# Sums of weights times the norm's shift taken as single columns, buffers zeroed at other places, and two steps of a long prologue in another order

## The chip, the cores and the metric

The kernel runs on one core of one Trainium2 chip. The metric is the device time of the whole launch in microseconds (us), the median of three runs. A core has TensorE (PE in the profile, with PEld for its weight loads), VectorE (DVE), ScalarE (ACT), GpSimd (POOL) and SyncE (SP, which here only issues transfers). All five run their own instruction streams and wait for one another by semaphores.

## The reference, cut to what matters

Two layers in float32 on a batch of 16 images of 192 channels and 56x56 points. The first is a Swin block: layer norm, attention in shifted windows of 7x7 with 6 heads of 32, a projection, a second layer norm and an MLP of 768 hidden channels. The second is a depthwise 3x3 convolution whose taps are computed from the pooled image (it isn't touched by the change).

```python
h = _ln(transpose(x, (0, 2, 3, 1)), norm1_g, norm1_b)      # over the 192 channels
h = roll(h, (-3, -3), axis=(1, 2))
win = windows_of_7x7(h)                                    # (16*64, 49, 192)
q, k, v = split(win @ qkv_w + qkv_b);  q = q * 32 ** -0.5
attn = q @ k.T + rel_bias[REL_IDX] + mask                  # mask: windows cut by the roll
out = softmax(attn) @ v @ proj_w + proj_b
x1 = x + roll_back(out)
y = gelu(_ln(x1, norm2_g, norm2_b) @ fc1_w + fc1_b) @ fc2_w + fc2_b
x2 = x1 + y
# then the dynamic depthwise convolution of x2
```

_ln(x, g, b) is (x - mean) / sqrt(var + 1e-5) * g + b. The kernel takes the mean, g and b out of the loop: with W the weights behind the norm, g goes into the rows of W once (the "fold"), the mean over the channels is taken out of the columns of the folded W once (the "centre"), and what b contributes, the sum over the channels of W[c, n] * b[c], is a constant for each column n that is added to the bias. That constant is what the kernel calls the shift. Of the norm itself there remains only one factor per token, 1/sqrt(var + eps).

## The kernel before, as far as the change and the steps touch it

The work is cut into 64 steps: four to an image, each of 7 rows of the upper half of the image and the same 7 of the lower half (T = 7 * 56 = 392 tokens a half). A software pipeline starts with a long prologue (steps 0 and 1, a part of step 2, and all weights), then comes a loop `for i in range(2, NS + 2)`, and an end. The edits all lie in the prologue. A tile has a place of its own or shares one by its tag; PSUM is cut into four pairs of banks, numbered 0 to 3, and `banks(name, k)` takes pair k as soon as those who used it before are done.

The helpers for the weights. The shift is a row: the vector be is spread over 128 columns and is the stationary operand, the raw weights stream past, and every row of the result is the sum. ACT copies row 0 out of PSUM, and `turn_row` then makes columns of it by products with a 1x1 operand.

```python
def fold_scale(raw, g, dst, groups):
    for to, lo, n, factor in groups:
        for c in range(2):
            d, r = dst[:, c, to : to + n], raw[:, c, lo : lo + n]
            if factor == 1.0:
                nc.vector.tensor_scalar(d, r, g[c], None, ALU.mult)
            else:
                nc.vector.tensor_scalar(d, r, g[c], factor, ALU.mult, ALU.mult)

# [...]
def shift(dst, raw, n, be, name):


    for c in range(2):
        cs = slice(c * n // 2, (c + 1) * n // 2)
        mm(dst[:, c, : n // 2], be[0].broadcast_to([128, 128]), raw[:, 0, cs], True, False)
        mm(
            dst[:, c, : n // 2],
            be[1][0:64].broadcast_to([64, 128]),
            raw[0:64, 1, cs],
            False,
            True,
        )
    row = one.tile([1, 2, n // 2], F32, tag="o", name=name)
    nc.scalar.copy(row, dst[0:1, :, : n // 2])
    return row.rearrange("o c n -> o (c n)")

def turn_row(dst, row, lo, n):
    mm(dst, row[:, lo : lo + n], ident[0:1, 0:1], True, True)
```

The start of the program, with the loads and the two tables for the attention scores: rel_r (the relative bias as each window token sees it, loaded by 14 small transfers, 7 for each of two windows) and mask_t. `biases` adds the two and so makes bias_t, which the first scores need. `norm_squares` squares x, `norm_stats` sums x and its squares over the channels on PE, `norm_vars` makes the variance, `norm_root` the root; the factors of step 0 are spread over the partitions by a product (pd), those of later steps by a trip through DRAM (`norm_spread`: rows out, dv back in, both by transfers). `norm1_scale` multiplies x by the factors into the window tiles win0 and win1.

```python
# [...] constants, loads of x and of the weights
nc.sync.dma_start(mask_t, win_mask)

side = 2 * WS - 1
for j in range(2):
    for yq in range(WS):
        q = j * 64 + yq * WS
        nc.gpsimd.dma_start(
            rel_r[q : q + WS].rearrange("p (y x) h -> p y (x h)", y=WS),
            bass.AP(
                rel_bias.tensor,
                yq * side * HEADS,
                [[HEADS, WS], [side * HEADS, WS], [1, WS * HEADS]],
            ),
        )
nc.gpsimd.memset(win0, 0.0)
nc.gpsimd.memset(win1, 0.0)
rel_hk = rel_r[:, ::-1, :].rearrange("p k h -> p h k")
# [...] rel_hk, biases()
g1, be1, bq, bk, bv = columns(*rows1, 2, nc.vector.tensor_copy)
norm_squares("1_0", 0, 0, nc.scalar, ("yn0", "q4"))
fold_scale(
    raw,
    g1,
    wqkv,
# [...] five blocks, with the scale for q
    ),
)
st = banks("st_a", 3)
keys = {0: "1_0"}
norm_stats(keys, {0: 0}, st)
part, _ = norm_vars(keys, st, "o")
norm_root(part)
nc.vector.reciprocal(part, part)
norm_squares("1_1", 1, 0, nc.scalar)
pm = fold_means(wqkv, 3 * DIM, "fq", 0)
pq = banks("qkb_p", 2)
row = shift(pq, raw, 3 * DIM, be1, "qkb_row")
pq = pq[:, 0, 384:390]
norm_squares("1_2", 2, 1, nc.scalar)

pd = banks("dv_0", 3)
for h in range(2):
    pick_row = ident[64:96, 64 + h * 16 : 65 + h * 16].broadcast_to([32, 128])
    mm(pd[:, h, :T], pick_row, part, True, True)
fold_center(wqkv, 3 * DIM, pm)
parts = (
    (qkb[:, 0:1], 0, 0, 0, 128, bq[0]),
    (qkb[:, 1:2], 1, 0, DIM, 128, bk[0]),
    (qkb[0:64, 2:3], 2, 0, 128, 64, bq[1][0:64]),
    (qkb[64:128, 2:3], 2, 64, DIM + 128, 64, bk[1][64:128]),
    (bv[0], 3, 0, 2 * DIM, 128, bv[0]),
    (bv[1][0:64], 4, 0, 2 * DIM + 128, 64, bv[1][0:64]),
)
for _, c, at, lo, n, _ in parts:
    turn_row(pq[at : at + n, c : c + 1], row, lo, n)
g2, be2, f2b, pb, cb = columns(*rows3, 1, nc.scalar.copy)
norm1_scale(0, pd[:, :, :T], nc.vector)
for dst, c, at, _, n, b in parts:
    nc.vector.tensor_tensor(dst, b, pq[at : at + n, c : c + 1], ALU.add)
nc.vector.tensor_scalar(qkb[:, 0:1], qkb[:, 0:1], SCALE, None, ALU.mult)
nc.vector.tensor_scalar(qkb[0:64, 2:3], qkb[0:64, 2:3], SCALE, None, ALU.mult)
nc.vector.tensor_scalar(kb, pick, qkb[:, 1:2], None, ALU.mult)
biases(0, 0)
nc.gpsimd.memset(kbd, 0.0)
for t in vbd:
    nc.gpsimd.memset(t, 0.0)
for t in prob:
    nc.gpsimd.memset(t, 0.0)
```

kbd, vbd and prob are block-diagonal or padded operands: their zeros are written once here, and later only the blocks are. After that come the statistics of steps 1 and 2, the attention of step 0, and steps 1 and 2 as far as the loop expects them:

```python
st = banks("st_b", 0)
keys = {0: "1_1", 1: "1_2"}
norm_stats(keys, {0: 1, 1: 2}, st)
part, _ = norm_vars(keys, st)
norm_root(part)
table(AF.Exp)
biases(0, 1)
nc.vector.reciprocal(part, part)
dvs.update(norm_spread(keys, part, tags=("dv1", "yn0"), order=(0, 1)))
images[1] = load_x(1, nc.sync)
biases(1, 0)
biases(1, 1)
# [...] 12 small loads by gpsimd
qs[0], outs = attention_qk(0, 1, 2, 3)
pvs, v_rest, v_whole = attention_v(0, (0, 1))
v_rest()
v_whole()
for f in outs:
    f()
fold_scale(rawf, g2, wf1, ((0, 0, HID, 1.0),))
attention_v_out(pvs)
norm1_scale(1, dvs.pop(0), nc.gpsimd)
# [...] 7 more loads by gpsimd
top, share = attention_scores(0, *qs.pop(0), (3, 2, 0, 1))
pv = banks("pb_p", 3)
pbp, f1p, pt = pv[:, 0, 384:386], pv[:, 0, 392 : 392 + NFC], pv[:, 1, 384:512]
top(0)
row = shift(pv, rawf, HID, be2, "f1b_row")

def rows_to_columns():
    for f in range(NFC):
        turn_row(f1p[:, f : f + 1], row, f * 128, 128)

qs[1], outs = attention_qk(1, 2, 0, 1, rows_to_columns, nc.vector)
# [...] proj bias
top(1)
share(0)
top(2)
share(1)
top(3)
share(2)
share(3)
norm_squares("1_3", 3, 0, nc.gpsimd)
outs[0]()
outs[1]()
prts = [attention_turn(0, wp, (2, 1)[wp % 2]) for wp in range(4)]
outs[2]()
outs[3]()
o = attention_rows(0, attention_values(0, prts, 3, 2))
# [...]
top, share = attention_scores(1, *qs.pop(1), (1, 0, 2, 3))
pvs, v_rest, v_whole = attention_v(1, (1, 0))
v_rest()
v_whole()
# [...] projection of step 0, scores
attention_v_out(pvs)
norm1_scale(2, dvs.pop(1), nc.gpsimd)
pm = fold_means(wf1, HID, "ff", 1)
top(2)
residual(0, pp, pair1)
norm_squares("2_0", 0, 1, nc.scalar)
st = banks("st_c", 0)
keys = {0: "1_3", 1: "2_0"}
norm_stats(keys, {0: 3, 1: 0}, st)
qs[2], outs = attention_qk(2, 2, 1, 3, None, nc.vector)
share(1)
fold_center(wf1, HID, pm)
top(3)
share(2)
share(3)
part, _ = norm_vars(keys, st)
table(AF.Sqrt)
norm_root(part)

s, m, g, b = (bn[:, k] for k in range(4))
nc.scalar.activation(s, s, AF.Sqrt, bias=eps_t)
nc.vector.reciprocal(part, part)
dvs.update(norm_spread(keys, part))
outs[0]()
outs[1]()
prts = [attention_turn(1, wp, (2, 3)[wp % 2]) for wp in range(4)]
outs[2]()
outs[3]()
o = attention_rows(1, attention_values(1, prts, 2, 3))
pvs, v_rest, v_whole = attention_v(2, (0, 1))
v_rest()
v_whole()
copies, sums_, squares, fold = norm_folded("1_4", 4, 0)
copies()
squares(nc.scalar)()
table(AF.Gelu)
sums_()
yns[0] = norm2_scale(0, dvs.pop(1), True)
fold()
# [...] fold, attention_v_out, projection of step 1, end of the norms
pairs = [0, 1, 2, 3]

for i in range(2, NS + 2):
```

`attention_qk` makes q, k and a mixed tile e by short products (64 channels) and long ones (128), with what it is given as `between` in their middle, and hands back four functions that copy the results out of PSUM. `attention_v_out` copies v into vbd, one half by DVE and one by ACT.

## Time and profile before

| | before |
|---|---|
| device time, median of 3 | 3050.23 us (3049.95 to 3051.91) |
| span of the profiled execution | 3046.8 us |
| share of the span that PE / DVE / ACT / POOL are busy | 99% / 71% / 64% / 44% |
| first product of the loop (ph) starts | 98.51 us |
| last row of POOL's zeroing | 14.96 to 22.39 us |
| first product for step 1 (pq) starts on PE | 43.70 us |
| mean clock granted to PE | 0.998 |

All times within the span count from its first instruction. Rows in the order of time give start, duration, engine, the line of the kernel, the operation, the tile written and the tile read, the shape, and how many neighbouring instructions are put together; a bracket gives the idle time before and what ended it. Rows of a stretch give its sum and then the busy time and count for PE, PEld, DVE, ACT and POOL, the clock granted to PE as a share of full speed, and what the transfers moved. The engines' names with a q stand for their queues that issue transfers.

### The profile page before, as it was taken

How to read it: one execution, taken by the hardware profiler on the slowest of the kernel's cores; microseconds unless marked ns; L12 is line 12 of the kernel's file. 1: busy time of each engine (PE TensorE's matmuls, PEld its weight loads, DVE VectorE, ACT ScalarE, POOL GpSimd, SP SyncE). 2: the span in 40 equal slices, each digit the busy share in tenths (PEclk: the TensorE clock that was granted, in tenths of full speed). 3: DMA queues.
4: the chain of work that ended last, by engine and by line, in shares of the span. 5: the costliest groups of instructions: out<-in, count | busy, mean ns of one | idle time of the engine just before them, and what ended most of it. 6: DMA issues, size and time to landing. Idle time of an engine off the chain costs nothing.

```text
span 3046.8 us, 62149 instructions
## 1 busy us (share of the span) xinstructions
PE 3021.9 (99%) x25174; PEld 1892.6 (62%) x25174; DVE 2156.5 (71%) x3840; ACT 1947.1 (64%) x3159; POOL 1345.4 (44%) x1270
## 2 busy tenths in 40 slices
PE   8999999999999999999999999999999999999998
PEld 5666666666666666666666666666666666666654
DVE  8666676676676676766866767767767668667664
ACT  4665676676666666766756667667666666666563
POOL 6434544434435345444444354453444444543422
PEclk9999999999999999999999999999999999999999
DMA  4102121121211112121121211212111121111101
GB/s 111 33 31 59 41 68 45 42 65 44 75 38 62 52 44 67 39 78 35 42 67 47 70 36 52 65 41 77 39 44 59 46 73 38 62 52 43 33 30 56
DMA packets 68710, 159.87 MB, mean 52 GB/s; under 512 B 11250, under 2 KB 35288, under 8 KB 66504
## 3 DMA queue, kind: packets, MB, share of 16 engines
q1 hardware_dynamic: 66766, 153.84, 16.6%
q8 instruction: 198, 3.24, 0.4%
q0 software_dynamic: 1360, 1.26, 0.3%
q14 instruction: 88, 0.72, 0.1%
q10 hardware_dynamic: 298, 0.81, 0.1%
HBM read 92.24 MB, written 38.93 MB: 43 GB/s over the span
## 4 chain that ended last, share of the span: by engine, by line
PE 97%; DVE 1%; POOL 1%; DMA 0%; issue 0%; ACT 0%; POOLq 0%; DVEq 0%; ACTq 0%
PE ph L87 26%; PE pf L87 25%; PE pv L87 8%; PE pp L87 8%; PE po L87 6%; PE pq L87 5%; PE pt L575 5%; PE sc L87 4%; PE pk L87 4%; PE pe L87 4%; PE st L87 2%; PE pc L87 0%; DVE e L553 0%; DVE bias_t L905 0%; PE pb_p L87 0%
## 5 line engine op out<-in xcount | busy, mean ns | idle before, releaser
L87 PE MATMUL pf<-hid,wf 128*128 128x392 f32 (+1 forms) x3072 | 802.7, 494 | 1.5 <-DVE e L546 1.5
L87 PE MATMUL ph<-yn,wf 128*128 128x392 f32 (+1 forms) x3072 | 799.1, 497 | 0.3 <-DVE x L651 0.3
L562 POOL TENSOR_TENSOR prob<-e,tot 113x588 f32<-113x588 f32 x256 | 298.2, 1176 | 1096.8 <-DVE tot L561 1096.7
L87 PEld LDWEIGHTS ph<-yn,wf 128*128 128x128 f32 (+1 forms) x3072 | 427.0, 188 | 344.1 <-issue 46.9
L87 PEld LDWEIGHTS pf<-hid,wf 128*128 128x128 f32 (+1 forms) x3072 | 386.9, 164 | 300.7 <-issue 119.8
L518 ACT COPY vbd<-pv 49x192 f32<-49x192 f32 x512 | 160.1, 313 | 576.7 <-DVE vbd L518 572.2
L711 DVE SCALAR_TENSOR_TENSOR x<-pf,cols,x 128x784 f32<-128x784 f32 (+1 forms) x128 | 106.2, 830 | 507.2 <-PE pf L87 453.3
L665 ACT ACTIVATE hid<-ph,f1b 128x784 f32<-128x784 f32 x384 | 336.8, 913 | 134.1 <-PE ph L87 132.6
L775 DVE SCALAR_TENSOR_TENSOR y<-x,wt,y 128x770 f32<-128x770 f32 x282 | 287.3, 1028 | 15.3 <-ACT y L767 7.0
L87 PEld LDWEIGHTS pv<-wqkv,win 64*128 64x128 f32 (+1 forms) x2048 | 255.5, 189 | 30.7 <-issue 1.2
L87 PE MATMUL pv<-wqkv,win 64*128 64x192 f32 (+1 forms) x2048 | 272.2, 325 | 0.0
L553 DVE TENSOR_TENSOR e<-e,top 113x588 f32<-113x588 f32 x256 | 261.7, 1022 | 8.9
L290 POOL TENSOR_TENSOR xs<-x,x 64x392 f32<-64x392 f32 x246 | 249.0, 1012 | 34.7 <-DVE x L651 25.5
L87 PE MATMUL pp<-o,wp 128*128 128x392 f32 (+2 forms) x896 | 251.4, 514 | 0.0
L581 ACT COPY prt<-pt 128x678 f32<-128x678 f32 x256 | 179.2, 726 | 111.3 <-PE pt L575 109.8
L257 ACT ACT_TABLE_LOAD x192 | 246.3, 1283 | 5.2 <-issue 1.8
L556 ACT ACTIVATE e<-e 113x588 f32<-113x588 f32 x256 | 177.1, 692 | 110.9 <-DVE e L553 110.9
L546 DVE TENSOR_TENSOR e<-sc,bias_t 113x588 f32<-113x588 f32 x256 | 179.4, 762 | 60.7 <-PE sc L87 59.7
L411 POOL TENSOR_TENSOR yn<-x,dv 128x784 f32<-128x784 f32 x62 | 116.1, 1872 | 234.6 <-DMA dv<-rows 234.6
L575 PEld LDWEIGHTS pt<-ident,prob 113*128 113x128 f32 x1536 | 165.5, 141 | 65.5 <-issue 36.3
L87 PE MATMUL po<-prt,vbd 128*64 128x49 f32 x6144 | 197.1, 224 | 0.5 <-ACT prt L581 0.5
L87 PEld LDWEIGHTS po<-prt,vbd 128*64 128x64 f32 x6144 | 188.9, 138 | 9.7 <-ACT prt L581 0.6
(185 smaller groups left out, 4440.1 us busy)
## 6 DMA issues: line engine op xcount, KB each, us to landing
dv<-rows SPq DMA_DIRECT2D x127, 392.0 KB
xs<-x SPq DMA_DIRECT2D x246, 98.0 KB
...
```

What stands on the lines that cost most here:

```text
L87: nc.tensor.matmul(dst, lhs, rhs, start=start, stop=stop, skip_group_check=True)
L257: nc.scalar.activation(junk, eps_t[0:1], func)
L290: nc.gpsimd.tensor_tensor(xs[p, 0], v0[p, h], v1[p], ALU.add)
L518: copy(dst, src[s * 64 : s * 64 + N, h, :, :, j, :])
L546: nc.vector.tensor_tensor(e, sc[:PW, :, : HEADS * N], rel, ALU.add)
L553: nc.vector.tensor_tensor(ehs[wp], ehs[wp], t.broadcast_to([PW, 2 * HEADS, N]), ALU.subtract)
L556: nc.scalar.activation(es[wp], es[wp], AF.Exp)
L562: nc.gpsimd.tensor_tensor(prob[wp][:PW, :, 0:N], ehs[wp], t.broadcast_to([PW, 2 * HEADS, N]), ALU.mult)
L575: nc.tensor.transpose(pt[:, a, g * PW : (g + 1) * PW], prob[wp][:PW, h : h + 2, :].rearrange("p h k -> p (h k)"), ident[:PW, :PW],)
L581: nc.scalar.copy(prt, pt[:, :, : 3 * PW])
L665: nc.scalar.activation(hid[:, f], phs[f][:, :, :T], AF.Gelu, bias=f1b[:, f : f + 1])
L775: nc.vector.scalar_tensor_tensor(dst, src, wt[:, kc, t : t + 1], dst, ALU.mult, ALU.add)
```

## The change

Its parts:

1. The shift becomes a column at once. The raw weights are the stationary operand and be is a single streamed column; two products give up to 128 sums, one in each partition, where they are wanted. The row, ACT's copy and `turn_row` go. For fc1 three of six columns are made ahead of the short products of step 1 and three in their middle.
2. Zeros are written in stretches in which the engine has nothing else to do: kbd by DVE right after the first columns; vbd and prob by GpSimd behind the first seven loads of rel_r, win0 and win1 ahead of them.
3. The other seven loads of rel_r are issued by ACT, after the squares of step 0.
4. The fold of the fc1 weights goes from DVE to ACT, behind the copies of v.
5. Steps 1 and 2: the statistics of steps 3 and 0 (st_c) come in the middle of the products for step 2, no longer ahead of them; q is copied before the root; the reciprocal and the trip of the factors come before the next copies, and the turned probabilities of step 1 use bank pairs 2 and 0; a root for the batch norm comes later, and the sums for step 4 are cut in two around the scaling of step 0.

It is meant to shorten the prologue: fewer products and copies, no wait of one engine for another's zeroing, and factors that are on their way earlier.

```diff
@@
 
 
 
-    def fold_scale(raw, g, dst, groups):
+    def fold_scale(raw, g, dst, groups, engine=nc.vector):
         for to, lo, n, factor in groups:
             for c in range(2):
                 d, r = dst[:, c, to : to + n], raw[:, c, lo : lo + n]
-                if factor == 1.0:
+                if engine is nc.scalar:
+                    nc.scalar.activation(d, r, AF.Copy, scale=g[c])
+                elif factor == 1.0:
                     nc.vector.tensor_scalar(d, r, g[c], None, ALU.mult)
                 else:
                     nc.vector.tensor_scalar(d, r, g[c], factor, ALU.mult, ALU.mult)
@@
             dv = dst[:, c].rearrange("p (c n) -> p c n", c=2)
             nc.vector.tensor_tensor(dv, dv, pm[:, :, : n // 2], ALU.subtract)
 
[... - shift and turn_row as shown above]
+    def shift(dst, raw, be, lo, n):
+
+        mm(dst, raw[:, 0, lo : lo + n], be[0], True, False)
+        mm(dst, raw[0:64, 1, lo : lo + n], be[1][0:64], False, True)
 
     ident = const.tile([128, 128], F32, tag="ident", name="ident")
     eps_t = const.tile([128, 1], F32, tag="eps", name="eps_t")
@@
             nc.sync.dma_start(xs[0:64, 1], v0[64:128, 0])
             nc.sync.dma_start(xs[64:128, 1], v0[0:64, 1])
 
-        def sums():
-            for p, h in own:
-                nc.gpsimd.tensor_tensor(xs[p, 0], v0[p, h], v1[p], ALU.add)
-            nc.gpsimd.tensor_tensor(xs[:, 0], xs[:, 0], xs[:, 1], ALU.add)
+        def sums(parts=(0, 1)):
+            if 0 in parts:
+                for p, h in own:
+                    nc.gpsimd.tensor_tensor(xs[p, 0], v0[p, h], v1[p], ALU.add)
+            if 1 in parts:
+                nc.gpsimd.tensor_tensor(xs[:, 0], xs[:, 0], xs[:, 1], ALU.add)
 
         def squares(engine):
             def those_of(dst, src):
@@
     nc.sync.dma_start(mask_t, win_mask)
 
     side = 2 * WS - 1
-    for j in range(2):
+
+    def rel_load(j, queue):
         for yq in range(WS):
             q = j * 64 + yq * WS
-            nc.gpsimd.dma_start(
+            queue.dma_start(
                 rel_r[q : q + WS].rearrange("p (y x) h -> p y (x h)", y=WS),
                 bass.AP(
                     rel_bias.tensor,
@@
                     [[HEADS, WS], [side * HEADS, WS], [1, WS * HEADS]],
                 ),
             )
+
     nc.gpsimd.memset(win0, 0.0)
     nc.gpsimd.memset(win1, 0.0)
+    rel_load(0, nc.gpsimd)
+    for t in (*prob, *vbd):
+        nc.gpsimd.memset(t, 0.0)
     rel_hk = rel_r[:, ::-1, :].rearrange("p k h -> p h k")
 
     def biases(r, e):
@@
 
 
     g1, be1, bq, bk, bv = columns(*rows1, 2, nc.vector.tensor_copy)
+    nc.vector.memset(kbd, 0.0)
     norm_squares("1_0", 0, 0, nc.scalar, ("yn0", "q4"))
+    rel_load(1, nc.scalar)
     fold_scale(
         raw,
         g1,
@@
     nc.vector.reciprocal(part, part)
     norm_squares("1_1", 1, 0, nc.scalar)
     pm = fold_means(wqkv, 3 * DIM, "fq", 0)
-    pq = banks("qkb_p", 2)
-    row = shift(pq, raw, 3 * DIM, be1, "qkb_row")
-    pq = pq[:, 0, 384:390]
+    pq = banks("qkb_p", 2)[:, 0]
+    parts = (
+        (qkb[:, 0:1], 0, 0, 0, 128, bq[0]),
+        (qkb[:, 1:2], 1, 0, DIM, 128, bk[0]),
+        (bv[0], 3, 0, 2 * DIM, 128, bv[0]),
+        (qkb[0:64, 2:3], 2, 0, 128, 64, bq[1][0:64]),
+        (qkb[64:128, 2:3], 2, 64, DIM + 128, 64, bk[1][64:128]),
+        (bv[1][0:64], 4, 0, 2 * DIM + 128, 64, bv[1][0:64]),
+    )
+    for _, c, at, lo, n, _ in parts:
+        shift(pq[at : at + n, c : c + 1], raw, be1, lo, n)
     norm_squares("1_2", 2, 1, nc.scalar)
 
     pd = banks("dv_0", 3)
@@
         pick_row = ident[64:96, 64 + h * 16 : 65 + h * 16].broadcast_to([32, 128])
         mm(pd[:, h, :T], pick_row, part, True, True)
     fold_center(wqkv, 3 * DIM, pm)
-    parts = (
-        (qkb[:, 0:1], 0, 0, 0, 128, bq[0]),
-        (qkb[:, 1:2], 1, 0, DIM, 128, bk[0]),
-        (qkb[0:64, 2:3], 2, 0, 128, 64, bq[1][0:64]),
-        (qkb[64:128, 2:3], 2, 64, DIM + 128, 64, bk[1][64:128]),
-        (bv[0], 3, 0, 2 * DIM, 128, bv[0]),
-        (bv[1][0:64], 4, 0, 2 * DIM + 128, 64, bv[1][0:64]),
-    )
-    for _, c, at, lo, n, _ in parts:
-        turn_row(pq[at : at + n, c : c + 1], row, lo, n)
     g2, be2, f2b, pb, cb = columns(*rows3, 1, nc.scalar.copy)
     norm1_scale(0, pd[:, :, :T], nc.vector)
     for dst, c, at, _, n, b in parts:
@@
     nc.vector.tensor_scalar(qkb[0:64, 2:3], qkb[0:64, 2:3], SCALE, None, ALU.mult)
     nc.vector.tensor_scalar(kb, pick, qkb[:, 1:2], None, ALU.mult)
     biases(0, 0)
-    nc.gpsimd.memset(kbd, 0.0)
-    for t in vbd:
-        nc.gpsimd.memset(t, 0.0)
-    for t in prob:
-        nc.gpsimd.memset(t, 0.0)
 
 
     st = banks("st_b", 0)
@@
     v_whole()
     for f in outs:
         f()
-    fold_scale(rawf, g2, wf1, ((0, 0, HID, 1.0),))
     attention_v_out(pvs)
+    fold_scale(rawf, g2, wf1, ((0, 0, HID, 1.0),), nc.scalar)
     norm1_scale(1, dvs.pop(0), nc.gpsimd)
     w2v = w2.rearrange("(c t) r -> c t r", t=9)[:, 0:NTAP, :]
     b2v = b2.rearrange("(c t) -> c t", t=9)[:, 0:NTAP]
@@
     pv = banks("pb_p", 3)
     pbp, f1p, pt = pv[:, 0, 384:386], pv[:, 0, 392 : 392 + NFC], pv[:, 1, 384:512]
     top(0)
-    row = shift(pv, rawf, HID, be2, "f1b_row")
-
-    def rows_to_columns():
-        for f in range(NFC):
-            turn_row(f1p[:, f : f + 1], row, f * 128, 128)
-
-    qs[1], outs = attention_qk(1, 2, 0, 1, rows_to_columns, nc.vector)
+
+    def shifts(fs):
+        for f in fs:
+            shift(f1p[:, f : f + 1], rawf, be2, f * 128, 128)
+
+    shifts(range(3))
+    qs[1], outs = attention_qk(1, 2, 0, 1, lambda: shifts(range(3, NFC)), nc.vector)
 
     mm(pbp[:, 0:1], wp0[:, 0:C0], bv[0], True, False)
     mm(pbp[:, 0:1], wp1[0:64], bv[1][0:64], False, True)
@@
     norm_squares("2_0", 0, 1, nc.scalar)
     st = banks("st_c", 0)
     keys = {0: "1_3", 1: "2_0"}
-    norm_stats(keys, {0: 3, 1: 0}, st)
-    qs[2], outs = attention_qk(2, 2, 1, 3, None, nc.vector)
+    qs[2], outs = attention_qk(
+        2, 2, 1, 3, lambda: norm_stats(keys, {0: 3, 1: 0}, st), nc.vector
+    )
     share(1)
     fold_center(wf1, HID, pm)
     top(3)
@@
     share(3)
     part, _ = norm_vars(keys, st)
     table(AF.Sqrt)
+    outs[0]()
     norm_root(part)
+    nc.vector.reciprocal(part, part)
+    dvs.update(norm_spread(keys, part))
+    outs[1]()
+    prts = [attention_turn(1, wp, (2, 0)[wp % 2]) for wp in range(4)]
 
     s, m, g, b = (bn[:, k] for k in range(4))
     nc.scalar.activation(s, s, AF.Sqrt, bias=eps_t)
-    nc.vector.reciprocal(part, part)
-    dvs.update(norm_spread(keys, part))
-    outs[0]()
-    outs[1]()
-    prts = [attention_turn(1, wp, (2, 3)[wp % 2]) for wp in range(4)]
     outs[2]()
     outs[3]()
     o = attention_rows(1, attention_values(1, prts, 2, 3))
@@
     copies()
     squares(nc.scalar)()
     table(AF.Gelu)
-    sums_()
+    sums_((0,))
     yns[0] = norm2_scale(0, dvs.pop(1), True)
+    sums_((1,))
     fold()
     attention_v_out(pvs)
     pp, pair1, p_narrow, p_rest, p_whole = project(1, o, 3, 2)
```

## The prediction, made before the changed kernel was run

> **What bounds the kernel now.** I read the page's busy shares first, then the stretches of the span, then the order in time of the first 100 us, because every line that changes belongs to the part ahead of the loop.
>
> The page, engines:
> ```profile
> PE 3021.9 (99%) x25174; PEld 1892.6 (62%) x25174; DVE 2156.5 (71%) x3840; ACT 1947.1 (64%) x3159; POOL 1345.4 (44%) x1270
> ```
> Busy time by stretch (us, then busy and count of PE, PEld, DVE, ACT, POOL, then clock and DMA):
> ```profile
> 0.00:26.00 26.00, 17.41 (x72) 7.17 (x72) 17.56 (x54) 7.25 (x13) 24.09 (x41) 0.87 0.70 162
> 26.00:41.00 15.00, 13.67 (x161) 9.35 (x154) 14.64 (x38) 11.30 (x21) 6.66 (x10) 1.00 0.57 144
> 41.00:59.00 18.00, 17.67 (x174) 12.54 (x175) 14.16 (x27) 8.77 (x12) 13.72 (x22) 1.00 0.44 115
> 59.00:77.00 18.00, 17.26 (x188) 10.34 (x186) 16.48 (x32) 7.19 (x16) 8.06 (x14) 1.00 0.00 1
> 77.00:98.50 21.50, 20.10 (x191) 14.09 (x188) 14.02 (x25) 16.00 (x30) 9.69 (x10) 1.00 0.15 49
> 98.50:3046.00 2947.50, 2935.83 (x24409) 1839.11 (x24407) 2079.64 (x3666) 1896.60 (x3067) 1283.17 (x1176) 1.00 0.17 51
> ```
> From 98.5 us on PE is busy 2935.8 of 2947.5 us and nothing there is edited: that stretch keeps its length. So the change can only move the moment at which the loop's first product (ph, 98.51 us in the chain of waits) starts, and a microsecond gained there is a microsecond of the total. Two per cent would be 61 us; the whole part ahead of the loop is 98.5 us and PE is busy 96.1 us of it (sum of the first five rows). Neither "faster" nor "slower" by 2% is in reach.
>
> Inside those 98.5 us the idle PE lies before 26 us (8.6 us). The order in time shows why:
> ```profile
> 14.96 2.08 POOL L965 MEMSET kbd<- 128x2352 f32 x1
> 16.95 2.72 POOL L967 MEMSET vbd<- 128x1536 f32 x2
> 19.59 2.80 POOL L969 MEMSET prob<- 128x768 f32 x4
> ...
> 16.02 6.42 DVE L138 COPY cols_rows<-cols_rows 5x64 f32<-5x64 f32 x1
> 17.02 5.42 DVE L387 TENSOR_TENSOR win<-x,dv 128x343 f32<-128x343 f32 x2
> ...
> 25.59 1.50 DVE L905 TENSOR_TENSOR bias_t<-rel_r,mask_t 113x98 f32<-113x98 f32 x6 [0.35 <-DMA wp<-in_L_conv_proj_w_dram]
> ```
> A copy of 5x64 elements "takes" 6.42 us: it starts under the row of seven memsets on POOL and ends (22.44) when they do (22.39). The first 5x64 copy of the kernel took 0.23. Three window products behind it still start (17.02 to 17.87) and end with it; the fourth comes only at 22.54, 0.42 apart it would have come at 18.29. So this stall costs DVE 4.25 us, and DVE is busy without a gap from there to the bias sums at 25.59 (call that moment B) and on to the scores.
>
> Two more lines matter because they lie on what comes next:
> ```profile
> DMA packets 85, 0.07 MB, mean 22 GB/s; under 512 B 1, under 2 KB 85, under 8 KB 85
> ...
> 33.57 0.82 SPq L362 DMA_DIRECT2D dv<-rows  x2
> ...
> 37.34 1.81 POOL L387 TENSOR_TENSOR win<-x,dv 128x343 f32<-128x343 f32 x2 [8.27 <-DVE vbd L518]
> ...
> 43.70 0.59 PE L87 MATMUL pq<-win,wqkv 64*128 64x392 f32 x1
> ```
> The first is the DMA view of 19.8 to 22.8 us: all it moves is the mask table, 28 packets a microsecond one after another (its 113 packets of 784 bytes end at 22.7, the last landing mark is 23.18). B waits for it, hidden until now. The others are one string: the norm factors of step 1 land at 37.17 (landing mark), POOL scales the window of step 1 from 37.34 to 43.65, and PE's product for step 1 starts at 43.70.
>
> [...]
>
> **The change part by part.**
> (a) Columns instead of rows. The row for qkb took 12.61 to 15.33 (2.72 us) plus turning 17.63 to 18.95 (1.32) and an ACT copy (0.63); that for f1b 40.86 to 43.69 (2.83), turning 1.42, copy 0.79. The new form is 12 products of one column each, 24 records. The kernel has the like already: pb from wp, 12 records in 1.40 us, so 24 take 2.8. PE is spared 1.3 and 1.45 us. Neither is on the path: at 15.4 PE waits for the norm factor anyway, and the second is followed by the wait for the window of step 1 (43.70).
> (b) Zeroing. kbd goes to DVE into the gap 4.66 to 7.79: 2352 elements at the 0.30 us of 294 give 2.4, ending at 7.1, free. POOL now does win (1.5 us) first, then 7 bias loads at 0.59 (4.15), so prob and vbd run from about 9.8 to 15.3 and no longer on the small copy. Gain: the 4.25 us stall.
> (c) The other 7 bias loads are issued by ACT between the squares and the statistics. [...]So ACT takes up the statistics at about 12.2 and not 9.35. Following it down: difference 12.8, root done 13.9, reciprocal (2.59) 16.5, two centre subtractions (1.4) 18.0, window (3.05) 21.3, or 22.5 if PE's clock is halved under dv, qkb sums (0.95) 22.3 to 23.5. It gives back about 1.8 us of (b).
> (d) SP's loads of x [...]shift by about 1 us, the mask with them: landing 23.7 to 24.0. B then comes at 24.2, bound by the mask, against 25.59: 1.4 gained out of 4.25.
> (e) Fold of wf to ACT: 1.13 us off DVE before the vbd copies. Last score product of step 0 at B+13.4 and no longer B+14.6: 37.6 against 40.20, 2.6 gained. But the window of step 1 hangs on B alone: reciprocal end B+6.25, factors landed B+11.6, POOL B+11.75 to B+18.1 = 42.3, perhaps 0.3 more since DVE's subtractions now fall on POOL's last pieces. PE starts at 42.3 to 42.6 against 43.70: 1.1 to 1.4 gained; the rest turns into PE idling before it.
> (f) From there to 73 us nothing changes its order, all shifts by the same.
> (g) Step 2 with its short products before the statistics st_c. In the old time scale: pq can start at 74.35 (POOL's window ends 74.34), pe must wait for DVE's centre subtraction of wf (76.22, same bank), pk ends 77.6, st_c (2.1) 79.7, long products (4.2) 83.9 against 83.05: 0.85 later. The first turnings gain it back: pt_1 waited 0.6 us for the kbd copies (bank 3) and now takes st_c's bank; on ACT q, root, kbd, four copies end at 88.2 and po ends at 90.3 against 90.37. The factors for yn land 2.1 us later (91.1 to 92) but yn is needed at 98.35 only. Sum: 0, give or take 0.7.
> Total: 1.2 gained, 3050.2 - 1.2 = 3049.0.
>
> **The rivals.**
> 1. [...]POOL's memsets (9.8) begin while DVE is in the last five folds of wqkv (to 10.78). If POOL gets in between two folds, they stand until 15.3, the means end at 19.0, the columns at 21.8, dv at 23.4, window and sums at 27.4, B near 27.9: 2.3 lost, about 3052.5. For it: POOL held on through seven instructions. Against: DVE's folds also follow without gap, and POOL's bias load at 10.21 took 0.69 instead of 0.59 and ended 0.12 after DVE's last fold, as if DVE held on.
> 2. ACT's issues do not wait long[...] and the mask is early: B near 22.5, the whole string 3 us earlier, 3047. Against: raw and step 1 landed at 8.9 and 11 and the issue order is fixed.
> 3. All is hidden: something after 59 us, such as (g) with 0.85 not regained or the folded sums of step 1 on POOL (which end at 107.18 just as PE asks for them), eats the rest: 3050 to 3051.
>
> **Range and chances.** I weigh the main line at 0.6, rival 1 at 0.25, the better case at 0.15: 0.6 of -1.2, 0.25 of +2.3, 0.15 of -3 is -0.6; with the median nearer the main line I say 3049.2. Three runs before spread by 2 us, so the range is 3046.3 to 3052.6. Both outer chances are nil but for error: 0.003 each.
>
> **What would show it.** The 5x64 copy near 18 us with 0.2 us; POOL's prob memset near 9.8 and no fold of wqkv of over 0.4 us (else rival 1); ACT's square of st_a near 12.2 (c); the first bias sum near 24.2 and the mask's landing just before (d); POOL's window of step 1 from 36 to 42.4 with PE waiting for it (e); pe of step 2 waiting for DVE's wf (g); ph near 97.3. Wrong if the ACT loads land late enough to hold the bias sums themselves, or if the loop shifts.

## The result, and the profile after

The changed kernel takes 3062.28 us, the median of 6 runs (3061.97 to 3064.40); the kernel before took 3050.09 beside it (6 runs, 3048.56 to 3051.91). The ratio is 1.0042 with a 95% interval of 1.0029 to 1.0055: slower by 12 us, where 1 us less was predicted and 3046.3 to 3052.6 was the range. Of the 13.7 us by which the profiled span grew (3046.8 to 3060.5), 12.2 lie ahead of the loop: its first product, ph, starts at 110.55 and not at 98.35 (this is the start of its record; 98.51, in the table before the change, is its place in the chain of waits).

First the page's engines, in the changed kernel:

```profile
PE 3030.6 (99%) x25182; PEld 1898.1 (62%) x25182; DVE 2161.3 (71%) x3839; ACT 1950.9 (64%) x3159; POOL 1340.3 (44%) x1262
```

PE does not idle more, it is busy for 8.7 us more, with 8 product records more in all. So it runs slower. The stretches of the changed kernel (columns as before: the stretch, its length, then busy time and count for PE, PEld, DVE, ACT and POOL, PE's clock, and the transfers) show where:

```profile
0.00:26.00 26.00, 15.48 (x49) 8.56 (x50) 17.72 (x32) 6.53 (x11) 21.16 (x38) 0.76 0.76 167
26.00:41.00 15.00, 15.00 (x70) 6.77 (x69) 11.38 (x42) 6.10 (x10) 0.00 (x0) 0.73 0.01 2
41.00:59.00 18.00, 15.34 (x156) 11.89 (x153) 16.48 (x35) 9.82 (x19) 13.31 (x22) 0.87 0.77 223
59.00:77.00 18.00, 17.52 (x270) 14.47 (x270) 9.64 (x18) 7.56 (x11) 4.20 (x4) 0.94 0.01 3
77.00:98.50 21.50, 18.67 (x95) 9.39 (x94) 17.55 (x33) 12.53 (x23) 12.36 (x18) 1.00 0.00 1
```

The reader should look at the clock: 0.76, 0.73, 0.87, 0.94, where the kernel before had 0.87 and then 1.00 throughout. In the second row PE is "busy" 15.00 of 15.00 us and gets through 70 product records; before, it got through 161 (not all of the same products) in 13.67. The record of the granted clock has it at half from 13.49 to 33.97, from 51.04 to 54.45 and from 57.86 to 61.28; in the kernel before only from 18.91 to 25.74.

What set this off stands in the order in time (start, duration, engine, line, operation, tiles, count; idle time before and its end in brackets), changed kernel:

```profile
4.15 1.45 DVE L138 COPY cols_rows<-cols_rows 5x64 f32<-5x64 f32 x1 [1.67 <-DMA cols_rows<-in_L_conv_qkv_b_dram]
6.57 2.02 DVE L910 MEMSET kbd<- 128x2352 f32 x1 [0.44 <-issue]
8.50 6.74 DVE L160 TENSOR_SCALAR wqkv<-raw,cols 128x128 f32<-128x128 f32 x2
9.66 2.79 POOL L890 MEMSET prob<- 128x768 f32 x4
12.33 0.48 ACT L334 ACTIVATE dev<-st_a 32x392 f32<-32x392 f32 x1 [6.16 <-DMA rel_r<-in_L_conv_rel_bias_dram]
12.38 2.72 POOL L890 MEMSET vbd<- 128x1536 f32 x2
15.85 4.62 PE L87 MATMUL fq_m<-wqkv,ones 128*128 128x288 f32 x7 [5.10 <-DVE wqkv L160]
20.88 4.95 PE L87 MATMUL qkb_p<-cols,raw 128*128 128x1 f32 x24
28.84 0.94 DVE L376 TENSOR_TENSOR win<-x,dv 128x343 f32<-128x343 f32 x2 [6.34 <-PE dv L87]
33.35 1.47 DVE L899 TENSOR_TENSOR bias_t<-rel_r,mask_t 113x98 f32<-113x98 f32 x6 [0.42 <-issue]
```

Two folds "take" 6.74 us and end with the row of memsets (15.10). PE gets nothing for 5.1 us, its clock halves, and the products that it then owes run at half speed: the means until 20.88, 24 columns until 25.75, dv until 28.7. The window of step 0 starts at 28.84, 11.8 us later than before, where it was then held to 22.44; the first bias sum (B) is 7.8 later. Further on:

```profile
45.24 1.82 POOL L376 TENSOR_TENSOR win<-x,dv 128x343 f32<-128x343 f32 x2 [23.03 <-PE sc L87]
51.17 1.79 PE L87 MATMUL pq<-win,wqkv 64*128 64x392 f32 x3 [1.36 <-POOL win L384]
55.34 1.94 PE L87 MATMUL pb_p<-cols,raw 128*128 128x1 f32 x12
57.20 2.37 PE L87 MATMUL pq<-win,wqkv 128*128 128x392 f32 x4
59.36 2.43 PE L87 MATMUL pk<-win,wqkv 128*128 128x392 f32 x4
61.64 1.48 PE L87 MATMUL pe<-win,wqkv 128*128 128x392 f32 x4
```

Four long products of the same shape take 2.37 and 2.43 us with most of their time at half clock, and 1.48 at full. To see which stretch loses what, three marks are enough, from the starts in each trace: the first pq of step 1, the first score of step 1, and ph.

| kernel | pq of step 1 | to the first score | from there to ph | ph |
|---|---|---|---|---|
| before | 43.70 | 15.56 | 39.09 | 98.35 |
| changed | 51.17 (+7.5) | 19.36 (+3.8) | 40.02 (+0.9) | 110.55 (+12.2) |

The last 1.45 us of the longer span come after ph: from there to the end it is 2949.92 us, before 2948.47. The stretches of the end, the kernel before first and then the changed one, have nearly the same work (36 PE records and 32) at another clock (0.91 and 0.79):

```profile
3027.00:3046.80 19.80, 12.24 (x32) 6.79 (x32) 13.54 (x17) 5.66 (x6) 3.52 (x4) 0.91 0.37 122
```
```profile
3039.00:3060.40 21.40, 13.73 (x36) 7.55 (x35) 13.91 (x18) 5.68 (x7) 3.53 (x4) 0.79 0.35 113
```

### The profile page after: what moved, and what is told of

The parts are those of the page before. It is cut to its first block, busy times and chain, and to the rows that moved or that the text cites. A ratio compares the mean times of both kernels' runs of the same rounds, so it can differ in the third digit from the quotient of the medians.

```text
span 3060.5 us, 62162 instructions
## 1 busy us (share of the span) xinstructions
PE 3030.6 (99%) x25182; PEld 1898.1 (62%) x25182; DVE 2161.3 (71%) x3839; ACT 1950.9 (64%) x3159; POOL 1340.3 (44%) x1262
## 4 chain that ended last, share of the span: by engine, by line
PE 96%; DVE 2%; DMA 1%; ACT 0%; issue 0%; POOL 0%; SPq 0%; POOLq 0%; DVEq 0%; ACTq 0%
PE ph L87 26%; PE pf L87 24%; PE pv L87 8%; PE pp L87 8%; PE po L87 6%; PE pq L87 5%; PE pt L564 5%; PE sc L87 4%; PE pk L87 4%; PE pe L87 4%; PE st L87 2%; PE pc L87 0%; DMA dv<-rows 0%; DVE wqkv L160 0%; DVE e L542 0%
## 5 line engine op out<-in xcount | busy, mean ns | idle before, releaser
L764 DVE SCALAR_TENSOR_TENSOR y<-x,wt,y 128x770 f32<-128x770 f32 x282 | 287.8, 1030 | 15.3 <-ACT y L756 7.0
```

The costliest lines, as they stand in the source:

```text
L764: nc.vector.scalar_tensor_tensor(dst, src, wt[:, kc, t : t + 1], dst, ALU.mult, ALU.add)
```

## The experiments

Each is one edit against a kernel that is named. The ratio is to runs of the kernel before on the same chip; its interval is the 95% one. The marks are those of one profiled execution of each kernel, the median is that of all its executions. They don't always agree: e3's profiled execution took 3055.42 us, 2.7 more than its median, and those of e14, e15 and e8 took 1.5 to 1.8 less than theirs.

| run | pq of step 1 | to first score | to ph | ph | median us | ratio, interval |
|---|---|---|---|---|---|---|
| e1_tt_folds | 44.66 | 21.83 | 40.71 | 107.20 | 3057.17 | 1.0025, 1.0014 to 1.0036 |
| e2_cols_after_dv | 50.05 | 17.49 | 40.61 | 108.15 | 3059.68 | 1.0039, 1.0024 to 1.0054 |
| e3_loads_pool | 41.66 | 21.77 | 42.22 | 105.65 | 3052.68 | 1.0011, 1.0005 to 1.0018 |
| e4_f1_ahead | 52.31 | 15.66 | 42.46 | 110.43 | 3060.54 | 1.0035, 1.0023 to 1.0046 |
| e5_loads_pool_row | 41.76 | 15.34 | 40.50 | 97.60 | 3048.62 | 0.9998, 0.9990 to 1.0007 |
| e6_loads_pool_row_order | 41.85 | 15.23 | 39.10 | 96.18 | 3046.86 | 0.9994, 0.9985 to 1.0002 |
| e7_loads_pool_fill | 42.59 | 15.68 | 43.07 | 101.34 | 3051.05 | 1.0004, 0.9996 to 1.0013 |
| e8_before_actcopy | 42.24 | 15.98 | 39.10 | 97.32 | 3049.53 | 1.0003, 0.9994 to 1.0012 |
| e9_extra_columns | 41.78 | 41.66 | 39.08 | 122.52 | 3073.49 | 1.0079, 1.0062 to 1.0096 |
| e10_extra_wide | 41.96 | 22.96 | 39.08 | 104.00 | 3054.21 | 1.0018, 1.0011 to 1.0025 |
| e11_best | 43.35 | 15.85 | 39.10 | 98.30 | 3049.10 | 0.9999, 0.9991 to 1.0008 |
| e12_best_b | 41.59 | 15.98 | 39.09 | 96.66 | 3048.19 | 0.9997, 0.9988 to 1.0005 |
| e13_row_actcopy_mask | 42.57 | 15.55 | 39.08 | 97.20 | 3046.94 | 0.9992, 0.9983 to 1.0000 |
| e14_zero_loads_only | 52.91 | 15.37 | 39.08 | 107.36 | 3059.26 | 1.0033, 1.0021 to 1.0045 |
| e15_qkb_row | 41.48 | 15.23 | 39.10 | 95.81 | 3047.67 | 0.9993, 0.9985 to 1.0001 |
| e6_again | 41.80 | 15.83 | 39.09 | 96.72 | 3046.91 | 0.9993, 0.9985 to 1.0001 |

### Is it the zeroing that holds the folds?

e1: the changed kernel with the folds in a form with two operands in SBUF.

```diff
-                elif factor == 1.0:
-                    nc.vector.tensor_scalar(d, r, g[c], None, ALU.mult)
                 else:
-                    nc.vector.tensor_scalar(d, r, g[c], factor, ALU.mult, ALU.mult)
+                    nc.vector.scalar_tensor_tensor(
+                        d, r, factor, g[c].broadcast_to([128, n]), ALU.mult, ALU.mult
+                    )
```

> The changed kernel with one edit: VectorE's ten folds of wqkv are written as scalar_tensor_tensor with the factor column spread over the elements[...]; everything else, GpSimd's zeroing under them too, stays. Theory 1[...]: the folds no longer wait, each takes 0.3 to 0.5 us, the last ends near 12 to 13 (raw's second half lands at about 9.6), the first mean product starts near 11 and not 15.85, the window of step 0 starts at 23 to 24 and not 28.84, ph near 105 to 107 and not 110.55; time about 3057. Theory 2 (the folds are late because their data are: the loads that ACT now issues delay raw): the folds still end after 16 and the time stays at 3062.

```profile
8.51 1.94 DVE L158 SCALAR_TENSOR_TENSOR wqkv<-raw,cols 128x128 f32<-128x128 f32 x10
9.65 2.79 POOL L890 MEMSET prob<- 128x768 f32 x4
12.37 2.71 POOL L890 MEMSET vbd<- 128x1536 f32 x2
```

Ten folds in 1.94 us, the last of them beside the same memsets at the same time, where two in the form with one operand in SBUF took 6.74. Theory 2 falls: the data were there. Theory 1, that the memsets hold the folds of the old form, stands; why a second SBUF operand frees them was not shown. Means start at 10.29, the window of step 0 at 19.73, pq of step 1 at 44.66, 6.5 us earlier. But ph gains only 3.4: the stretch behind pq grew from 19.36 to 21.83, with the clock at half from 40.0 to 57.1. The median is 5.1 lower than that of the changed kernel, and still 8.1 above the kernel before. Something else takes the gain back.

A part of it stands ahead of pq. With the folds free, the first bias sum comes at 26.70, 1.1 later than before, because the mask is late:

```profile
26.70 1.49 DVE L899 TENSOR_TENSOR bias_t<-rel_r,mask_t 113x98 f32<-113x98 f32 x6 [2.88 <-DMA mask_t<-in_win_mask_dram]
```

The mask's 113 packets of 784 bytes end at 26.30 in the changed kernel; before they ended at 22.70. This comes with the seven loads on ACT: SP issues the mask at 17.53 in the changed kernel and at 17.74 in e1, but at 15.54 in e3 (below), which differs from the changed kernel by the queue of these loads alone, and at 15.93 in the kernel before. The changed kernel hides it behind the held folds.

e3: the changed kernel with all the small loads on GpSimd again, which moves the zeroing behind the folds (to 14.64).

```diff
     rel_load(0, nc.gpsimd)
+    rel_load(1, nc.gpsimd)
     for t in (*prob, *vbd):
...
-    rel_load(1, nc.scalar)
```

> The changed kernel with all 14 loads of the relative bias issued by GpSimd again, ahead of the zeroing of prob and vbd (undoes part c, and so puts the zeroing behind the folds). Theory 1[...]: raw lands near 8.9, the folds end by 11, GpSimd zeroes from about 14 to 19.5 and stalls the small copy and the first windows of step 0 as in the kernel before, for about 3 us; ph between 97 and 100, time 3049 to 3052. Theory 2 (columns and new order cost the time by themselves): ph stays above 104, time above 3056.

The folds ended at 10.67, the small copy was held for 3.86 us (16.26 to 20.12), the first bias sum came at 23.83 and pq of step 1 at 41.66, 2 us before the kernel before: up to here as theory 1, by which the held folds are the cause, has it. Yet ph came at 105.65, where it expected 97 to 100, and the median lies at 3052.68. So the zeroing (with the loads) is one cause and there is another, between pq of step 1 and ph. It is worth 9 us in this profiled execution and about 6 in the median, which lies 3.6 above the kernel before, if pq comes 2 us early in all executions.

e14: the other way round, the kernel before with the zeroing, the loads and the fold of wf as changed, but rows, turning and order as before.

```diff
+    rel_load(0, nc.gpsimd)
+    for t in (*prob, *vbd):
+        nc.gpsimd.memset(t, 0.0)
...
+    nc.vector.memset(kbd, 0.0)
...
+    rel_load(1, nc.scalar)
...
-    nc.gpsimd.memset(kbd, 0.0)
-    for t in vbd:
-        nc.gpsimd.memset(t, 0.0)
-    for t in prob:
-        nc.gpsimd.memset(t, 0.0)
```

> The kernel before with parts 2 to 4 of the change alone (zeroing at its new places, seven loads by ACT, the fold of wf on ACT): rows and turning as before, steps 1 and 2 in the old order. Theory 1[...]: the folds end near 16.7 as in the changed kernel, pq of step 1 starts at 48 to 51, from there to the first score of step 1 15.6 us as before, ph near 103 to 105: 5 to 6 of the 12 us; time about 3055. Theory 2[...]: ph at 110, time 3062.

Theory 1 takes the held folds for one cause beside columns and order, theory 2 for the only one. The kernel has the held folds (end 16.73) and half clock from 14.11 to 34.59, and no loss behind pq: 15.37 and 39.08. ph comes at 107.36, 9.0 later than before and not the 5 to 6 that I expected; the median is 3059.26. So the zeroing, with the loads, brings three quarters of the loss or more even without columns (9.0 of 12.2 us at ph, 9.7 of 12.2 in the medians). That is more than the 6.1 us by which the folds end later (16.73 against 10.67 in e3), as PE then has to catch up at half clock. Four kernels make a square; each field has ph, and behind it the median less that of the kernel before:

| ph; median less before, us | rows, old order | columns, new order |
|---|---|---|
| zeroing behind the folds | 95.81; -1.85 (e15) | 105.65; +3.63 (e3) |
| zeroing under the folds, 7 loads on ACT | 107.36; +9.74 (e14) | 110.55; +12.19 (changed) |

Against the best corner the zeroing with the loads alone costs 11.6 us at ph and in the medians, columns and order alone 9.8 at ph but 5.5 in the medians, and all together 14.7 and 14.0: they share waits and half clock, so that no shares can be given that add up. The kernels of e14 and e15 differ by one line, the queue that issues the seven loads, and that line is worth the 11.6 us: with all loads ahead of it the zeroing starts behind the folds.

e8: is the stall in the kernel before, the 4.25 us that the prediction wanted back, worth anything? The kernel before with the small copy of the second vectors on ACT:

```diff
-        nc.vector.tensor_copy(rows[:, DIM:256], rows[:, C0:DIM])
+        copy(rows[:, DIM:256], rows[:, C0:DIM])
```

> The kernel before with one edit: the copy of 5x64 elements behind the second set of vectors, which stood 6.42 us under GpSimd's zeroing, is done by ACT. Theory 1[...]: the windows of step 0 start at 17.0 and take 0.9 us for the first two, the last ends near 20.5 and not 24.2, st_b starts at about 19.2 and not 22.7, the first bias sum then waits for the mask at about 23.3 in place of 25.59; ph 1.5 to 3 us earlier, time about 3047.5. Theory 2 (the zeroing shuts out every VectorE instruction): the windows still stretch to 22.4, and the time stays at 3049.

```profile
16.87 2.72 POOL L967 MEMSET vbd<- 128x1536 f32 x2
17.15 0.94 DVE L387 TENSOR_TENSOR win<-x,dv 128x343 f32<-128x343 f32 x2 [0.92 <-PE dv L87]
18.79 0.23 ACT L138 COPY cols_rows<-cols_rows 5x64 f32<-5x64 f32 x1
23.30 1.48 DVE L905 TENSOR_TENSOR bias_t<-rel_r,mask_t 113x98 f32<-113x98 f32 x6 [0.96 <-DMA mask_t<-in_win_mask_dram]
```

The windows run under the memsets at 0.94 us for two, where the same two took 5.42 behind the held copy in the kernel before. So theory 2 falls, and of the instructions there only the copy had been held; the bias sums then wait for the mask, as the prediction's (d) had it. Of 4.25 us there remain 2.3 at B, 1.5 at pq of step 1 and 1.0 at ph in the profile, and none in the median (3049.53 against 3049.34 beside it). Single executions spread from 3047.4 to 3054.3; why they spread more than before was not settled.

### What is lost behind pq of step 1?

e2: the columns of qkb behind dv in the changed kernel.

```diff
-    for _, c, at, lo, n, _ in parts:
-        shift(pq[at : at + n, c : c + 1], raw, be1, lo, n)
...
     fold_center(wqkv, 3 * DIM, pm)   # after the products for dv
+    (the two lines, ahead of it)
```

> The changed kernel with the 24 column products for qkb put behind the four products that spread step 0's norm factors (dv), as the only edit. Theory 1 (the columns, at 0.2 us each on a PE at half clock, stand in the path ahead of dv): dv starts at 20.9 in place of 25.76, the window of step 0 near 24 in place of 28.84; the sums for qkb then wait for the columns, which end near 28.7, so the first bias sum comes at about 30 in place of 33.35 and ph 3 us earlier, near 107.5; time about 3059. Theory 2 (the columns stand beside another wait that ends no earlier): ph and time do not move by more than 1 us.

dv starts at 20.85, the window at 23.93, B at 30.09, as theory 1 says to a tenth, and the median is 3059.68, which the intervals don't tell from the changed kernel's. The columns at half clock did stand in the path; but a row there costs as much, since in e14 dv starts at 25.89 and the bias sums at 33.15. pq of step 1 gains only 1.1, and ph 2.4; behind pq the clock is at half once, from 61.96 to 65.37.

e4: all six columns of f1b ahead of step 1's products.

```diff
-    shifts(range(3))
-    qs[1], outs = attention_qk(1, 2, 0, 1, lambda: shifts(range(3, NFC)), nc.vector)
+    shifts(range(NFC))
+    qs[1], outs = attention_qk(1, 2, 0, 1, None, nc.vector)
```

> The changed kernel with all six columns of f1b made ahead of the products of step 1, where PE idles for the window (49.8 to 51.17), none in their middle. Theory 1 (the three in the middle are 1.9 us on PE's path, and the idle stretch ahead of them halves its clock): from the start of pq for step 1 to the first score of step 1 takes 2 to 4 us less than the 19.4 of the changed kernel; ph 2 to 4 us earlier, time about 3059. Theory 2 (that stretch is bound by VectorE and ACT): no change over 0.5 us.

The stretch fell to 15.66, 3.7 less, as theory 1 has it. But pq started 1.1 later, since the columns ran past the end of the wait, and the next stretch grew to 42.46 with half clock from 82.96 to 89.79: ph stayed at 110.43. A gain moved on and was lost again, at PE's clock both times (0.83 from pq to the first score in the changed kernel, and half for 6.83 us here).

Now three kernels on top of e3. e5 makes f1b's shift a row that is turned, as in the kernel before:

```diff
-    shifts(range(3))
-    qs[1], outs = attention_qk(1, 2, 0, 1, lambda: shifts(range(3, NFC)), nc.vector)
+    row = shift_row(pv, rawf, HID, be2, "f1b_row")
+    def rows_to_columns(): ...        # six turn_row, as before
+    qs[1], outs = attention_qk(1, 2, 0, 1, rows_to_columns, nc.vector)
```

> The changed kernel with all loads of the relative bias on GpSimd (as in the run of that name) and, besides, the shift of f1b as a row that is turned, as in the kernel before; columns remain for qkb. Theory 1 (PE's clock: the short columns leave PE idle in front of step 1's window, or do not count as activity, and the clock halves; the slower row kept PE busy): no half clock between 38 and 60 us, from the first pq of step 1 to the first score of step 1 about 15.6 us and not 21.8, ph near 99 to 100, time near 3049.5. Theory 2 (the clock halves there for another reason, such as the earlier window): the stretch stays above 19 us and the time at 3052 to 3053.

The stretch from pq to the first score, in e3 and then in e5:

```profile
41.66:63.43 21.77, 21.44 (x171) 15.74 (x171) 11.09 (x23) 7.60 (x11) 11.95 (x14) 0.72 0.26 61
```
```profile
41.76:57.10 15.34, 15.01 (x173) 12.03 (x171) 11.50 (x24) 8.16 (x12) 11.33 (x13) 1.00 0.36 85
```

The same number of products within two, at a clock of 0.72 and of 1.00: 6.4 us. ph moves by 8.05 between these two executions and the median by 4.1 (3052.68 to 3048.62), by an edit that gives PE more work.

e7 keeps the columns and fills the wait of 1.3 us ahead of pq:

```diff
     shifts(range(3))
+    for _ in range(2):
+        mm(pv[:, 1, 0:384], ones, rawf[:, 0, 0:384], True, True)   # read by nobody
```

> All loads on GpSimd, columns for f1b as in the changed kernel, and two products of 128x384 whose result nobody reads put behind the first three columns, to fill PE's wait for the window of step 1 (1.3 us). Theory 1a (it is the idle stretch that halves the clock): no half clock from 40 to 60 us, the stretch from pq to the first score 17.5 us (15.6 and the inline columns), ph near 101. Theory 1b (single-column products do not count as activity, and the clock halves by them): half clock still shows behind the columns, the stretch stays near 20 or above.

No half clock from pq to the first score, and 15.68 us. The median is 3051.05 against 3052.68; the two intervals overlap, but no execution of e7 lies above 3051.94, and e3's reach 3057.14. It looks as if the idle wait had halved the clock in e3. But e3's own rows say that the wait did not begin it:

```profile
37.74 0.73 PE L87 MATMUL sc<-kbd,q 64*64 64x98 f32 x24 [0.74 <-ACT vbd L507]
38.40 1.94 PE L87 MATMUL pb_p<-cols,raw 128*128 128x1 f32 x12
41.66 1.79 PE L87 MATMUL pq<-win,wqkv 64*128 64x392 f32 x3 [1.32 <-POOL win L384]
```

The clock is at half from 40.27, and the wait lasts from 40.34 to 41.66. I look at the 3.41 us ahead of such an edge because the edges in the changed kernel (13.49, 33.97, 51.04, 54.45, 57.86, 61.28) lie 3.41 us or multiples of it apart; that just this length counts is a guess of mine. The 3.41 us ahead of 40.27 hold columns (1.9 us) and an earlier wait (0.74). In the changed kernel columns alone were followed by half clock: the 3.41 us ahead of 57.86 hold the twelve of 55.34, and PE has no gap in them.

```profile
54.45:57.86 3.41, 3.41 (x19) 2.45 (x16) 3.31 (x7) 1.14 (x2) 3.35 (x5) 1.00 0.47 94
57.86:61.28 3.42, 3.42 (x6) 1.69 (x5) 0.46 (x2) 0.92 (x1) 3.42 (x4) 0.50 0.32 121
```

Idleness alone was, too, in a kernel below (e11), where half clock starts at 16.55 and the 3.41 us ahead of it hold a wait of 1.73 us and practically no column (the first starts at 16.54):

```profile
15.03 1.58 PE L87 MATMUL dv<-dev,ident 32*128 32x392 f32 x4 [1.73 <-DVE dev L949]
```

No limit can be read from this: in e7 the stretch from 39.28 to 42.69 holds as many columns as that of the changed kernel, and no half clock follows.

To see columns with nothing beside them, two kernels were made on top of e6, which does not idle at the place. e9 adds 48 single columns, e10 adds 11 wide products, both read by nobody:

```diff
+        for k in range(24):                                   # e9
+            shift(pv[:, 1, 16 * k : 16 * k + 1], rawf, be2, (k % NFC) * 128, 128)
...
+        for _ in range(11):                                   # e10
+            mm(pv[:, 1, 0:384], ones, rawf[:, 0, 0:384], True, True)
```

> The kernel with f1b as a row, all loads on GpSimd and the old order of steps 1 and 2 (the run of that name), with 48 single-column products nobody reads put in the middle of step 1's products, without any wait: 7.8 us of PE time at full clock (0.08 us a record as in the changed kernel). Theory 1b (single-column products do not count as activity for PE's clock): the window of 3.41 us behind them is at half clock, though PE never idles; from pq to the first score of step 1 over 24.5 us, where 15.2 and 7.8 make 23.0. Theory 1a (only idle stretches halve the clock): no half clock between 30 and 80 us, 23.0 us.

> The same with 11 products of 128x384 nobody reads in the same place, 7.8 us of PE time at full clock. Both theories: no half clock between 30 and 80 us, from pq to the first score of step 1 23.0 us; if the clock halves here too, the stretch costs for another reason than the kind of product, such as the longer wait of the other engines.

In e9, order in time and stretches:

```profile
44.09 1.49 PE L87 MATMUL pb_p<-ident,f1b_row 1*128 1x1 f32 x12
45.51 23.29 PE L87 MATMUL pb_p<-cols,raw 128*128 128x1 f32 x96
68.73 2.98 PE L87 MATMUL pq<-win,wqkv 128*128 128x392 f32 x4
```
```profile
40.00:47.60 7.60, 7.60 (x44) 5.77 (x42) 7.39 (x13) 2.77 (x4) 7.38 (x14) 1.00 0.79 156
47.60:75.00 27.40, 27.40 (x94) 23.92 (x94) 1.73 (x4) 2.18 (x3) 5.56 (x5) 0.50 0.04 17
```

In e10:

```profile
46.18 7.36 PE L87 MATMUL pb_p<-raw,ones 128*128 128x384 f32 x22
53.38 1.48 PE L87 MATMUL pq<-win,wqkv 128*128 128x392 f32 x4
```
```profile
46.20:53.40 7.20, 7.20 (x24) 4.29 (x24) 4.38 (x8) 0.88 (x2) 5.49 (x5) 1.00 0.28 83
```

PE is busy without a gap in both (27.40 of 27.40 us, 7.20 of 7.20). Under columns the clock halves 2.1 us behind their start (at 47.64; the twelve 1x1 products of 44.09 stand ahead of them) and stays at half for 27.3 us, 6 us beyond their end; under wide products it stays at 1.00, and the stretch is 22.96 us where 23.0 was expected. So half clock follows single-column products (27.3 us of it in e9) as it follows idleness (10.24 us in e11, behind a wait of 1.73). Which of their traits brings it was not separated: they stream few columns, and they load weights for most of the time (PEld is busy 23.92 of 27.40 us in e9, 4.29 of 7.20 in e10). The halved stretches last multiples of 3.41 us (27.3 is eight), and the busy time of the profile does not tell them from the others: it is 27.40 of 27.40 us at a clock of 0.50 in e9, and 7.20 of 7.20 at 1.00 in e10. What the clock follows was not shown beyond that. My size for e9 was off: a record of the columns takes 0.16 us at full clock (12 in 1.94) and not 0.08, so that 96 of them would be 15.5; they took 23.3 with most of them at half.

### What does the new order cost?

e6: on top of e5, the order of steps 1 and 2 put back.

```diff
-    qs[2], outs = attention_qk(
-        2, 2, 1, 3, lambda: norm_stats(keys, {0: 3, 1: 0}, st), nc.vector
-    )
+    norm_stats(keys, {0: 3, 1: 0}, st)
+    qs[2], outs = attention_qk(2, 2, 1, 3, None, nc.vector)
...  (root, reciprocal, factors, turned probabilities and sums as before)
```

> As the run before it, and the order of steps 1 and 2 (statistics st_c, root, reciprocal, turned probabilities, sums) put back as well, so that of the change only the columns for qkb, kbd's zeroing on VectorE, win's zeroing ahead and the fold of wf on ACT are left. Theory 1 (the new order costs by its waits: PE idles for POOL's window and for VectorE's centre of wf, and may halve its clock after them): from the first score of step 1 to ph 39.2 us as before and not 40 to 42; ph 1 to 3 us earlier than in that run, near 97; time 3048. Theory 2 (the order is neutral): no difference over 0.5 us.

ph comes 1.4 us earlier, and the median is 1.8 lower (3048.62 to 3046.86). In the table, all runs with the old order have 39.08 to 39.10 from the first score to ph, to 0.02 us; those with the new one have 40.0 to 43.1, over 42 where the clock halved in it (e3, e4, e7). What PE waits for in the changed kernel up to 111 us (us in total, times, longest):

```profile
PE pq L87 <- POOL win L384: 2.2, 2, 1.4
...
PE pe L87 <- DVE wf L174: 1.0, 1, 1.0
```

What is left of the 2.2 beside the longest is the wait for the window of step 2. In e6 neither the wait for that window nor the one for the centre of wf appears among PE's waits: there the products for st_c lie in the time in which both get done.

### A version that follows

e6 keeps of the change the columns for qkb, kbd's zeroing on VectorE, win's zeroing ahead and the fold of wf on ACT. Four kernels tried to go on from it.

e11 has the small copy on ACT, the mask's load ahead of the fc1 weights, and qkb's columns behind dv; e12 the same without the last; e15 is e6 with qkb as a row; e13 is e15 with the copy and the mask of e11.

```diff
-        nc.vector.tensor_copy(rows[:, DIM:256], rows[:, C0:DIM])
+        copy(rows[:, DIM:256], rows[:, C0:DIM])
...
+    nc.sync.dma_start(mask_t, win_mask)
     nc.sync.dma_start(rawf[:, 0], fc1_w[0:C0])
```

> The kernel with f1b as a row, all loads on GpSimd and the old order of steps 1 and 2, and besides: the small copy of the second set of vectors on ACT (so that GpSimd's zeroing shuts nothing out), the mask's load ahead of the fc1 weights, and the columns of qkb behind dv. If the causes found so far are right: dv at 15 in place of 16.6, first window of step 0 at 16.7 in place of 19.2, first bias sum at 21 to 22 in place of 23.55, pq of step 1 at 40 to 41 in place of 41.85, ph 1 to 2 us earlier than 96.18; time near 3045.5.[...]

> As the run before it, with the columns of qkb left ahead of dv. If the columns stand in the path there: dv at 16.6, window at 17.5 to 18, first bias sum at 22 to 23, ph 0.5 to 1 us later than in that run; if they stand beside another wait: the same ph within 0.3 us.

> The best version so far (f1b as a row, all loads on GpSimd, old order) with qkb as a row that is turned, too, so that no single-column products of the change are left. If the columns for qkb cost here as well: dv at 15.3 in place of 16.6, ph 0.5 to 1.5 us earlier than 96.18. If they stand beside the stall of the small copy (to 19.8 in both): ph within 0.5 us, the times the same.

> As the run before it, with the small copy of the second set of vectors on ACT and the mask's load ahead of the fc1 weights. If the causes found are all: dv at 15.2, first window of step 0 at 16.9, first bias sum at 21.5 to 22.5, pq of step 1 at 40 to 41, ph near 95; time near 3045.5.[...]

> The best version so far once more, with more rounds beside the two above: 3046.9, 2 to 2.5 us under the kernel before, ph near 96.2.

e11 missed. dv (15.03) and the window (16.71) came when they should, but PE idled for 1.73 us ahead of dv, the clock halved from 16.55 to 26.79, the columns behind dv took 4.95 us and pushed st_b to 21.71 from 20.05; pq of step 1 came at 43.35, later than in e6. e12 is no better than e6 either (ph 96.66, median 3048.19): its first window came at 19.22 and not at 17.5 to 18, and its first bias sum at 23.54, where e6 has 23.55. In e15 ph comes at 95.81, against 96.18 and 96.72 in two profiles of e6, and its median lies 0.8 above e6's beside it (3047.67 and 3046.91): no cost and no gain of qkb's columns can be told there. e13 missed 3045.5: its dv came at 16.65 and not at 15.2, the clock halved from 18.04, ph is 97.20, and its median (3046.94) is that of e6 beside it.

So e6 stands: 3046.86 and, on another chip, 3046.91, with the kernel before at 3049.34 and 3049.52 beside it. That is 2.5 and 2.6 us less; the intervals of the ratio reach 1.0002 and 1.0001, so the gain is not beyond doubt, though in the second comparison 12 of its 13 runs (3045.90 to 3047.88) lie under the lowest of 34 of the kernel before (3047.76).

## Why the prediction was wrong, point by point

- The sums. The first five rows of the stretches add up to 86.1 us of busy PE and not 96.1. So PE idles 12.4 us ahead of the loop, 8.6 of them before 26 us; this bears on no later step.
- The path. That only the prologue could move, and that ph's start carries over, held: 12.2 of 13.7 us. The other 1.45, half clock at the end, was not thought of; no run tested it alone.
- (b), the step that failed first. The zeroing of prob and vbd came at 9.66 to 15.10, as said (9.8 to 15.3), and left the small copy alone (0.17 us). But "free" and "Gain: the 4.25 us stall" were both wrong. win's zeroing held the first small copy (1.45 us, before 0.23), so kbd's zeroing ran from 6.57 to 8.59 and not to 7.1 (though it took 2.02 us and not 2.4) and pushed the first fold from 7.79 to 8.50. From there the folds of wqkv were held: the first two to 15.2 and the last to 16.74, where it had ended at 10.78. PE waited 5.1 us for them and went to half clock from 13.49 to 33.97, and B came at 33.35 and not at 24.2. With the zeroing and the loads alone (e14), ph came 9.0 us late; with the folds freed (e1), the means started at 10.29. The gain would have been small in any case: e8 takes the stall away and gains 1.0 us at ph and nothing in the median.
- Rival 1 named this, with 0.25 and 2.3 us. Its size failed mostly by half clock: it let the means end at 19.0, the columns at 21.8 and B come at 27.9; they came at 20.88, 25.75 and 33.35. The argument against it (a load that took 0.69 and not 0.59, "as if DVE held on") was read into a tenth of a microsecond.
- (a). The columns were mis-sized: 24 records were put at 2.8 us after pb's 1.40 for 12, of which ten load narrower weights or fewer rows. They took 3.16 for qkb at (nearly) full clock in e3, and 3.88 for f1b. Worse is "neither is on the path": qkb's stood between the reciprocal (20.61) and dv, where e14's row costs as much, and three of f1b's stood between products of step 1.
- (c) was right in time (ACT's seven issues lasted from 5.72 to 12.29 and its square came at 12.33, said 12.2), though by what rule they wait for other transfers was my assumption and was not shown. It was without effect, as VectorE took the difference only at 16.77, behind the folds.
- (d) was right that the mask comes later (SP issues it at 17.53 and not at 15.93, and stood 2.0 us waiting for rel_r) and that B would wait for it, and wrong in size: its packets end at 26.30 and not just before 24. The held folds hide it in the changed kernel, but in e1 B waits for it until 26.70. So even with the folds free, the gain of 1.4 us at B is a loss of 1.1 there.
- (e) was right: GpSimd's window starts at B + 11.9 (said 11.75), PE waits for it (1.36 us); the window took 6.64 us and not 6.31, as the 0.3 more allowed for: two pieces of 64x28 took 0.97 beside a subtraction of VectorE, and 0.55 before. What was not seen is what stands there in place of the slower row: twelve columns and this wait of 1.4 us fill the time from 47.87 to 51.17, and the clock is at half from 51.04.
- (f), "nothing changes its order, all shifts by the same": 19.36 in place of 15.56, through the half clock from 51.04 to 54.45 and from 57.86 to 61.28; with a row instead (e14) it was 15.37. This step lost most in e3's profile, 6.2 us.
- (g), "0, give or take 0.7": 0.9 in the changed kernel, 1.4 between e5 and e6, 3 and more with half clock.

One thing was left out of nearly all steps: I read PE's clock in the profile (0.87 in the first stretch) and took it as given, not as something that the change moves. Only (c) asks what half clock under dv would add (1.2 us).
